# A bilinear interaction kernel: x in a ring loaded two blocks at a time, products in place, engine orders as written

One core of one Trainium2 chip. The metric is the device time of one execution in microseconds, smaller is better. Times are medians of several executions, all with nothing else on the core.

## The reference

Every row of the batch has 32 vectors of 64 numbers. For each of the 496 pairs i < j, vector i is multiplied by the pair's own 64 x 64 matrix and the result, number by number, by vector j.

```python
# inputs: r_inputs (4096, 32, 64) f32, L0_rec_W (496, 64, 64) f32
idx_i, idx_j = np.triu_indices(32, k=1)
vi = inputs[:, idx_i, :]
vj = inputs[:, idx_j, :]
vidots = jnp.einsum('bpd,pde->bpe', vi, W)
return vidots * vj          # (4096, 496, 64) f32: 520 MB
```

## The kernel before

128 rows form a row tile, two row tiles (k = 0, 1) a block, 16 blocks the batch. A row tile's 496 pairs are cut into five groups; a group is computed into one of three output buffers (`ot`) and stored with one DMA of 2.9 to 3.4 MB. x comes in blocks, W is transposed once at the start ("order" rearranges a chunk, "turn" transposes it on TensorE). Seven of the 46 product steps of a row tile go "aside": ScalarE (ACT) copies the matmul result out of PSUM, GpSimd (POOL) multiplies. The others are multiplied by VectorE (DVE) straight from PSUM.

```python
xpool = ctx.enter_context(tc.tile_pool(name="xpool", bufs=2))
xtpool = ctx.enter_context(tc.tile_pool(name="xtpool", bufs=4))
tpool = ctx.enter_context(tc.tile_pool(name="tpool", bufs=4))
opool = ctx.enter_context(tc.tile_pool(name="opool", bufs=3))
psum = ctx.enter_context(tc.tile_pool(name="psum", bufs=4, space=bass.MemoryType.PSUM))
# ... (cut)
def order_w(c: int, k: int, copy):
    r = wrows[c][1] - wrows[c][0]
    rp = tpool.tile([P, EU, 2, D], F32, tag="tmp", name=f"rp_{c}_{k}")
    src = raw[c][:r, :].rearrange("p (d h e) -> p e h d", h=2, d=D)
    copy(rp[:r], src[:, k * EU : (k + 1) * EU])
    return rp
# ... (cut: turn_w, turn_x)
LEAD = 3    # the first three row tiles go group by group, the others one after the other
sched = [(t, s) for g in range(len(groups)) for t in range(LEAD) for s in range(NS) if steps[s][0] == g]
sched += [(t, s) for t in range(LEAD, NT) for s in range(NS)]
# ... (cut)
for c, orders, turns in (                     # at which step a quarter of a W chunk is
    (1, (2, 4, 8, 10), (4, 7, 12, 15)),       # ordered and turned
    (2, (17, 22, 27, 32), (19, 24, 29, 34)),  # chunk 2 is ordered on POOL
    (3, (54, 54, 55, 55), (57, 60, 63, 66)),
):
    ...
no_aside = range(52, 67)
# ... (cut: the loop over sched; per step the matmuls into ps, then)
if i in aside and c0 == 0 and s not in no_aside:
    tmp = tpool.tile([P, CH, 2, E2], F32, tag="tmp", name=f"tmp_{s}")
    nc.scalar.copy(tmp, src)
    nc.gpsimd.tensor_mul(dst, tmp, xj)
else:
    nc.vector.tensor_mul(dst, src, xj)
# after a group's last step: nc.sync.dma_start(out rows <- ot)
```

## Time and profile before

| | before |
|---|---|
| time | 1354.68 us (1354.08 to 1354.79) |
| span of the profiled execution | 1353.3 us |
| DMA | 562.9 MB, 416 GB/s over the span |
| PE, DVE, POOL, ACT busy | 87, 71, 39, 28% |
| stores | 161 on one queue, 520 MB |

The share of DMA engines busy is in tenths over 40 slices of the span, and it is 9 in all but the last; no compute engine comes near that. The lines themselves stand in the prediction. The trace also has a record of every DMA packet (queue, size, start, length, but no engine number); where this text says "packet records", its numbers were worked out from those.

### The profile page before, as it was taken

What the parts mean: (1) busy time and instruction counts of PE and PEld (TensorE: products, weight loads), DVE (VectorE), ACT (ScalarE), POOL (GpSimd) and SP (SyncE); (2) the same over time, 40 slices, a digit from 0 to 9 for tenths busy, and PEclk for the clock granted to TensorE, in tenths of its full rate; (3) what the DMA queues carried; (4) which work ended last, traced back from release to release, by engine and by line L of the source; (5) the groups of instructions that cost most, each with busy time, mean ns of one, the idle gap of its engine ahead of it and who ended that gap; (6) DMA issues with size and microseconds to landing.
All of it is one profiled execution on the core that took longest, in us unless ns stands there. A gap on an engine that the chain in (4) does not pass through costs nothing.

```text
span 1353.3 us, 17856 instructions
## 1 busy us (share of the span) xinstructions
PE 1180.3 (87%) x7424; PEld 690.9 (51%) x7424; DVE 956.9 (71%) x1262; ACT 374.1 (28%) x367; POOL 530.2 (39%) x246
## 2 busy tenths in 40 slices
PE   6989889889799897988879989888987989988994
PEld 4556545545455454555445545454554545545552
DVE  5778768767677676776757777676775767767774
ACT  3432222222232232222222222222222222223221
POOL 1813424444243443433444334433434434344431
PEclk9989999989999898999989999899998999989997
DMA  9999999999999999999999999999999999999997
GB/s 386 370 426 408 424 427 431 428 432 431 418 414 419 433 412 418 422 413 426 428 407 422 417 425 410 423 421 407 425 410 426 419 422 427 401 432 428 415 417 319
DMA packets 26273, 562.92 MB, mean 416 GB/s; under 512 B 2912, under 2 KB 2912, under 8 KB 3040
## 3 DMA queue, kind: packets, MB, share of 16 engines
q1 hardware_dynamic: 24048, 530.59, 92.4%
q10 hardware_dynamic: 2144, 31.20, 5.5%
q8 instruction: 58, 0.95, 0.3%
q14 instruction: 23, 0.19, 0.0%
HBM read 41.68 MB, written 520.09 MB: 415 GB/s over the span
## 4 chain that ended last, share of the span: by engine, by line
DMA 50%; PE 25%; DVE 17%; POOL 3%; issue 2%; ACT 0%; DVEq 0%; SPq 0%; POOLq 0%; ACTq 0%
DMA out_dram<-ot 50%; PE ps L211 20%; DVE ot L228 17%; PE ptx L114 4%; POOL ot L226 3%; PE ptw L104 1%; DMA raw<-in_L_rec_W_dram 1%; ACT tmp L225 0%; DVE rp L95 0%; POOL rp L95 0%; DVEq L228 0%; ACT wT L107 0%; SPq L76 0%; POOLq L226 0%; SPq L233 0%
## 5 line engine op out<-in xcount | busy, mean ns | idle before, releaser
L228 DVE TENSOR_TENSOR ot<-ps,xs 128x1024 f32<-128x1024 f32 (+15 forms) x1252 | 945.6, 808 | 364.7 <-DMA out_dram<-ot 185.9
L211 PE MATMUL ps<-wT,xT 64*128 64x512 f32 (+13 forms) x6272 | 1034.9, 473 | 132.8 <-DVE ot L228 121.3
L211 PEld LDWEIGHTS ps<-wT,xT 64*128 64x128 f32 x6272 | 563.7, 197 | 569.9 <-DVE ot L228 306.8
L226 POOL TENSOR_TENSOR ot<-tmp,xs 128x1024 f32<-128x1024 f32 x220 | 519.6, 2362 | 647.4 <-ACT tmp L225 457.1
L225 ACT COPY tmp<-ps 128x1024 f32<-128x1024 f32 x220 | 222.7, 1012 | 500.1 <-PE ps L211 459.6
L118 ACT COPY xT<-ptx 128x1024 f32<-128x1024 f32 x128 | 129.6, 1012 | 428.2 <-PE ptx L114 428.2
L114 PE MATMUL ptx<-ident,xs 128*128 128x128 f32 x1024 | 141.2, 281 | 18.5 <-DVE ot L228 9.9
L114 PEld LDWEIGHTS ptx<-ident,xs 128*128 128x128 f32 x1024 | 111.0, 142 | 64.3 <-issue 44.1
L72 POOL MEMSET xs<- 128x64 f32 x16 | 2.4, 152 | 148.6 <-DVE ot L228 148.6
L104 PE MATMUL ptw<-ident,rp 128*128 128x128 f32 (+1 forms) x128 | 19.2, 305 | 3.9 <-DVE rp L95 3.9
L104 PEld LDWEIGHTS ptw<-ident,rp 128*128 128x128 f32 (+1 forms) x128 | 16.2, 160 | 10.3 <-DVE rp L95 5.0
L107 ACT COPY wT<-ptw 128x1024 f32<-128x1024 f32 (+1 forms) x15 | 14.8, 984 | 21.4 <-PE ptw L104 21.4
L95 DVE COPY rp<-raw 128x1024 f32<-128x1024 f32 (+1 forms) x9 | 10.7, 1219 | 11.1 <-DMA raw<-in_L_rec_W_dram 11.1
L95 POOL COPY rp<-raw 128x1024 f32<-128x1024 f32 x4 | 8.0, 1994 | 0.1
L95 ACT COPY rp<-raw 112x1024 f32<-112x1024 f32 (+1 forms) x3 | 5.9, 1959 | 5.1 <-POOL ot L226 3.3
L107 DVE COPY wT<-ptw 128x1024 f32<-128x1024 f32 x1 | 1.2, 1224 | 3.3 <-PE ptw L104 3.3
L118 ACT ACT_TABLE_LOAD x1 | 1.3, 1283 | 0.7 <-PEq L251 0.7
masks.py:197 POOL MEMSET ident<- 128x128 f32 x1 | 0.2, 206 | 0.3 <-POOLq L251 0.3
masks.py:199 POOL TENSOR_SCALAR_AFFINE_SELECT ident<-ident 128x128 f32<-128x128 f32 x1 | 0.3, 295 | 0.0
L251 POOL MEMSET const-float32-0.0<- 128x1 f32 x1 | 0.1, 99 | 0.2 <-issue 0.2
L251 POOL MEMSET const-bfloat16-1.0<- 128x1 bf16 x1 | 0.1, 102 | 0.0
L251 POOL MEMSET const-uint8-127<- 128x1 uint8 x1 | 0.1, 102 | 0.0
(1 smaller groups left out, 0.1 us busy)
## 6 DMA issues: line engine op xcount, KB each, us to landing
out_dram<-ot SPq DMA_DIRECT2D x64, 3360.0 KB, 16.2
out_dram<-ot SPq DMA_DIRECT2D x32, 3168.0 KB, 15.4
out_dram<-ot SPq DMA_DIRECT2D x32, 3104.0 KB, 17.0
out_dram<-ot SPq DMA_DIRECT2D x31, 2880.0 KB, 16.4
xs<-in_r_inputs_dram ACTq DMA_DIRECT2D x14, 2048.0 KB, 16.6
raw<-in_L_rec_W_dram SPq DMA_DIRECT2D x3, 2048.0 KB, 14.3
xs<-in_r_inputs_dram SPq DMA_DIRECT2D x2, 1024.0 KB, 10.9
xs<-in_r_inputs_dram SPq DMA_DIRECT2D x1, 2048.0 KB, 24.6
```

What stands on the lines that cost most here:

```text
L72: nc.gpsimd.memset(xs[blk][:, 0, :], 0.0)
L95: copy(rp[:r], src[:, k * EU : (k + 1) * EU])
L104: nc.tensor.transpose(pt[:, n, :r], rp[:r, n].rearrange("p h d -> p (h d)"), ident[:r, :r])
L107: copy(wT[c][:, :, k * EU : (k + 1) * EU], pt[:, :, :r].rearrange("p e r -> p r e"))
L114: nc.tensor.transpose(pt[:, n, :], xs[blk][:, s : s + 2, :].rearrange("p f d -> p (f d)"), ident)
L118: copy(xT, pt)
L211: nc.tensor.matmul(ps[:, h, lo - pa : hi - pa, :], xT[blk, kt, n // RUN][h * D : (h + 1) * D, n % RUN, :], wT[c][h * D : (h + 1) * D, lo - ...
L225: nc.scalar.copy(tmp, src)
L226: nc.gpsimd.tensor_mul(dst, tmp, xj)
L228: nc.vector.tensor_mul(dst, src, xj)
L251: nc = _bacc.Bacc("TRN2", target_bir_lowering=False, num_devices=1)
```

## The change

x sits in one ring of three blocks, and two neighbouring blocks come by one load of 4 MB; where the ring puts the pair in swapped places, rows of the two blocks swap roles. The place of the ring that the first two blocks leave free (the middle one) holds the rearranged W at the start, so no temporary tiles are left. The last chunk of W is now loaded at step 36; before, its load stood behind the last copy of chunk 2, at step 32. An aside product is copied into the output buffer and multiplied there. No step is exempt from going aside. The instructions of each engine run in the order of the source, where before a scheduler ordered them.

```diff
-    xpool = ctx.enter_context(tc.tile_pool(name="xpool", bufs=2))
-    tpool = ctx.enter_context(tc.tile_pool(name="tpool", bufs=4))
+    NX = 3
+    xs = const.tile([P, 1 + NX * NB * F, D], F32, tag="xs", name="xs")
+    def slot(blk: int, k: int, i: int = 0) -> int:
+        c, n = divmod(blk, 2)
+        b = 1 - n if c % 2 else 2 * n if c == 0 else 1 + n
+        return 1 + (b * NB + k) * F + i
+    def load_two(blk: int, eng):
+        ...                                   # cut: one DMA for blocks blk, blk + 1
+        eng.dma_start(out=dst[:, b : b + 2, :], in_=src)
@@ order_w
-        rp = tpool.tile([P, EU, 2, D], F32, tag="tmp", name=f"rp_{c}_{k}")
+        rp = xs[:, 1 + NB * F : 1 + 2 * NB * F, :].rearrange("p (n e h) d -> p n e h d", e=EU, h=2)[:, k]
@@ steps of ordering, loads
-        (1, (2, 4, 8, 10), (4, 7, 12, 15)),
+        (1, (0, 0, 2, 6), (4, 7, 12, 15)),
-    no_aside = range(52, 67)
+    LAST_W = 36                               # the last chunk of W is loaded at this step
-    loads = {place[blk * NB, LATE]: blk + 1 for blk in range(2, NBLK - 1)}
-    loads[place[LEAD, LATE]] = 2
+    loads = {place[LEAD, LATE]: 2}
+    for blk in range(3, NBLK - 1, 2):
+        loads[place[blk * NB, LATE]] = blk + 1
+    ctx.enter_context(tc.manual_schedule())
@@ the product
-        if i in aside and c0 == 0 and s not in no_aside:
-            tmp = tpool.tile([P, CH, 2, E2], F32, tag="tmp", name=f"tmp_{s}")
-            nc.scalar.copy(tmp, src)
-            nc.gpsimd.tensor_mul(dst, tmp, xj)
+        if i in aside and c0 == 0:
+            nc.scalar.copy(dst, src)
+            nc.gpsimd.tensor_mul(dst, dst, xj)
```

More of the change, by code (lines that the diff above doesn't have):

```diff
@@ L62, with rows_in @@
     make_identity(nc, ident)
-    xs = {}
+    NX = 3
+    xs = const.tile([P, 1 + NX * NB * F, D], F32, tag="xs", name="xs")
+    nc.gpsimd.memset(xs[:, 0, :], 0.0)
     def rows_of(dram: bass.AP, blk: int) -> bass.AP:
         return dram[blk * NB * P : (blk + 1) * NB * P]
-    def new_x(blk: int):
-        xs[blk] = xpool.tile([P, 1 + NB * F, D], F32, tag="xs", name=f"xs_{blk}")
-        nc.gpsimd.memset(xs[blk][:, 0, :], 0.0)
-    def load_x(blk: int, eng, k0: int = 0, k1: int = NB):
-        src = rows_of(x, blk).rearrange("(p k) f d -> p (k f) d", k=NB)
-        eng.dma_start(out=xs[blk][:, 1 + k0 * F : 1 + k1 * F, :], in_=src[:, k0 * F : k1 * F, :])
+    def slot(blk: int, k: int, i: int = 0) -> int:
+        c, n = divmod(blk, 2)
+        b = 1 - n if c % 2 else 2 * n if c == 0 else 1 + n
+        return 1 + (b * NB + k) * F + i
+    def rows_in(dram: bass.AP, blk: int) -> bass.AP:
+        return rows_of(dram, blk ^ (blk // 2 % 2))
+    def load_x(blk: int, eng, k0: int = 0, k1: int = NB):
+        src = rows_in(x, blk).rearrange("(p k) f d -> p (k f) d", k=NB)
+        eng.dma_start(
+            out=xs[:, slot(blk, k0) : slot(blk, k1 - 1) + F, :], in_=src[:, k0 * F : k1 * F, :]
+        )
+    def load_two(blk: int, eng):
+        n = NB * F
+        dst = xs[:, 1:, :].rearrange("p (b n) d -> p b (n d)", n=n)
+        b = min(slot(blk, 0), slot(blk + 1, 0)) // n
+        src = x[blk * NB * P : (blk + 2) * NB * P].rearrange("(b p k) f d -> p b (k f d)", b=2, k=NB)
+        eng.dma_start(out=dst[:, b : b + 2, :], in_=src)
     wflat = w.rearrange("p d e -> p (d e)")
@@ L112, in turn_x @@
         for n in range(RUN):
-            s = k * F + q * RUN + n
+            s = slot(blk, k, q * RUN + n) - 1
             nc.tensor.transpose(
-                pt[:, n, :], xs[blk][:, s : s + 2, :].rearrange("p f d -> p (f d)"), ident
+                pt[:, n, :], xs[:, s : s + 2, :].rearrange("p f d -> p (f d)"), ident
             )
@@ L158 @@
             due.setdefault(turns[k], []).append(("turn", c, k))
-    no_aside = range(52, 67)
+    LAST_W = 36
     LATE = 6
-    loads = {place[blk * NB, LATE]: blk + 1 for blk in range(2, NBLK - 1)}
-    loads[place[LEAD, LATE]] = 2
-    new_x(0)
+    loads = {place[LEAD, LATE]: 2}
+    for blk in range(3, NBLK - 1, 2):
+        loads[place[blk * NB, LATE]] = blk + 1
     load_x(0, nc.sync, 0, 1)
@@ L169 @@
     load_w(2)
-    new_x(1)
     load_x(1, nc.sync)
+    ctx.enter_context(tc.manual_schedule())
     v, p, a = nc.vector.tensor_copy, nc.gpsimd.tensor_copy, nc.scalar.copy
@@ L185 @@
         g, i, c0, m = steps[st]
+        if s == LAST_W:
+            load_w(3, nc.scalar)
         if s in loads:
-            new_x(loads[s])
-            load_x(loads[s], nc.scalar)
+            load_two(loads[s], nc.scalar)
         for what, *args in due.get(s, ()):
@@ L196 @@
                 rps[c, k] = order_w(c, k, (v, v, p, v)[c] if k % 2 == 0 else (v, v, p, a)[c])
-                if (c, k) == (2, NU - 1):
-                    load_w(3, nc.scalar)
         base, end = groups[g]
@@ L218 @@
         o = pa - base
-        j = 1 + kt * F + i + 1 + c0
+        j = slot(blk, kt, i + 1 + c0)
         dst = ot[:, o : o + m, :].rearrange("p m (h e) -> p m h e", h=2)
         src = ps[:, :, :m, :].rearrange("p h m e -> p m h e")
-        xj = xs[blk][:, j : j + m, :].rearrange("p m (h e) -> p m h e", h=2)
-        if i in aside and c0 == 0 and s not in no_aside:
-            tmp = tpool.tile([P, CH, 2, E2], F32, tag="tmp", name=f"tmp_{s}")
-            nc.scalar.copy(tmp, src)
-            nc.gpsimd.tensor_mul(dst, tmp, xj)
+        xj = xs[:, j : j + m, :].rearrange("p m (h e) -> p m h e", h=2)
+        if i in aside and c0 == 0:
+            nc.scalar.copy(dst, src)
+            nc.gpsimd.tensor_mul(dst, dst, xj)
         else:
@@ L233 @@
             nc.sync.dma_start(
-                out=rows_of(out, blk).rearrange("(p k) n d -> p k n d", k=NB)[:, kt, n0 : pa + m, :],
+                out=rows_in(out, blk).rearrange("(p k) n d -> p k n d", k=NB)[:, kt, n0 : pa + m, :],
                 in_=ot[:, n0 - base : pa + m - base, :],
```

## The prediction

> **What bounds the kernel now.** I read the page's header, busy shares and DMA rows first, then the stretches, then the waits, and last the start of the chain that ended last. The page:
>
> ```profile
> span 1353.3 us, 17856 instructions
> PE 1180.3 (87%) x7424; PEld 690.9 (51%) x7424; DVE 956.9 (71%) x1262; ACT 374.1 (28%) x367; POOL 530.2 (39%) x246
> DMA  9999999999999999999999999999999999999997
> DMA packets 26273, 562.92 MB, mean 416 GB/s; under 512 B 2912, under 2 KB 2912, under 8 KB 3040
> q1 hardware_dynamic: 24048, 530.59, 92.4%
> q10 hardware_dynamic: 2144, 31.20, 5.5%
> ```
>
> No engine is full, and the 16 DMA engines are: q1 (stores, W and the first x) and q10 (x loads issued by ACT, and the last part of W) together take 97.9% of 16 engines' span. The bytes are the output's, so they can't shrink. In the trace's packet records the commonest store packet, 26880 bytes, takes 996 ns, 27.0 bytes/ns. An engine's share is 562.92/16 = 35.18 MB, 1303 us at that rate. So some 50 us of the span are not plain transfer. The stretches say where some lie (us from the start; the last columns are granted clock, DMA share, GB/s):
>
> ```profile
> 0.00:27.00 27.00, 15.66 (x82) 11.51 (x84) 11.16 (x11) 10.35 (x9) 3.28 (x9) 1.00 0.94 388
> 27.00:60.00 33.00, 33.00 (x199) 18.74 (x196) 24.78 (x25) 15.19 (x15) 23.38 (x11) 1.00 0.92 378
> 60.00:104.00 44.00, 40.22 (x255) 25.55 (x253) 32.93 (x41) 17.55 (x16) 12.76 (x7) 0.88 0.97 399
> 104.00:140.00 36.00, 35.51 (x250) 21.52 (x248) 30.50 (x48) 8.10 (x8) 9.53 (x5) 1.00 1.00 418
> 340.00:1340.00 1000.00, 880.09 (x5526) 510.80 (x5524) 714.17 (x950) 268.28 (x265) 398.31 (x179) 0.95 0.99 419
> 1345.00:1351.00 6.00, 0.00 (x0) 0.00 (x0) 0.00 (x0) 0.00 (x0) 0.00 (x0) 0.50 0.07 31
> ```
>
> The start, to about 104 us, is short of stores and PE is full in it (20.00 of 20 us, 33.00 of 33). The last row is the surprise: for 6 us the DMA share is 0.07, about one engine in sixteen (0.0625). The packet records agree: at the end most engines are done near 1344.3 us, one goes on to 1350.4. Following that one back: around 500 us it moves 23040 bytes in 860 to 898 ns where the others take 855, and 24832 in 935 to 982 where they take 921, with no gap between packets. **One DMA engine is 3 to 4% slower per packet.** Its distance behind the others grows from 1 us at 160 us to about 6 us at 330 us, and then stays there: an output buffer is free only when the slowest sixteenth of its store is done, so the other fifteen wait for it. The chain's starts of the matching stores confirm the pace: 431.27 and 514.33, 83.1 us for two row tiles of five stores each. At 27 bytes/ns the two tiles' 34.6 MB would be 80.1 us. So from about 104 us on the end is set by that engine's own work, whatever the compute engines do, as long as it never runs dry. That compute is ahead of it:
>
> ```profile
> DVE ot L228 <- DMA out_dram<-ot: 185.9, 84, 5.8
> POOL ot L226 <- DMA out_dram<-ot: 153.1, 59, 5.5
> ACT tmp L225 <- POOL ot L226: 36.1, 9, 5.0
> ```
>
> DVE waits 84 times for an output buffer, 186 us over 32 row tiles, 5.8 us a tile.
>
> **What the Trainium skill says.** (1) "DMA: Bandwidth & Descriptors", section "Latency and other measured facts": engines 7 and 15 are usually slower in traces, with a guessed cause tied to software descriptor rings. This trace has one slow engine; its records carry no engine number, and all queues that matter here are hardware ones, so the guessed cause does not fit. (2) Same page, "Measured": 425 GB/s for a 16 MB load on a lone core; the trace has 430 between 140 and 340 us. There is no rate left for larger loads to win. (3) Same page, "Issuing engines are not separate DMA queues": loads from ACT and stores from SP share the 16 engines and interleave. The trace agrees: while a load runs, packets of 16384 bytes (611 ns) and of 26880 alternate on the slow engine. So two blocks in one load move the same packets over the same engines.
>
> **The change, part by part.**
>
> *Loads.* 14 loads of 2 MB become 7 of 4 MB; packets stay 16 KB, 128 per block. Each issue costs ACT about 0.4 us, beside the path. I looked for a cost at each start of a load: stores' packets are late by 0.3 to 0.8 us there, but on the fast engines, which had just been idle (they have run out of stores); on the slow engine packets are only 50 to 70 ns late. Saving: 0 to 1 us. A pair arrives two tiles (about 83 us) less some steps before its first use, as before, and the order of instructions shows no new wait for a load. Expected cost 0. The 14 further memsets (0.15 us each) also go, off the path.
>
> *Aside products.* 220 become 224: ACT copy 1.01 us, POOL product 2.36 us. Four DVE products of 1.22 us move away, all in steps 52 to 66, where PE is the limit: about 0. The copies now go to the output buffer, so ACT itself waits for a store, in order, and transposed x behind it waits too. PE gets one or two PSUM steps less far ahead at the start of a group; I estimate 1 us a group, 4 us a tile, against DVE's 5.8 us of waiting. The slow engine has a queued store of some 8 us when a buffer comes free. So 0 in the end.
>
> *Orders.* PE's order is the same line for line, and DVE's differs in a handful of rows of the start. On POOL each of the four W reorderings for rows 256 to 383 moves behind one more product. The chain there was:
>
> ```profile
> 43.40 2.37 POOL ot L226
> 45.76 1.84 issue
> 47.64 2.35 POOL ot L226
> 49.99 1.94 POOL rp L95
> 51.92 2.33 POOL ot L226
> 56.12 2.42 POOL ot L226
> 58.55 16.29 DMA out_dram<-ot
> ```
>
> I redo it with the new order, ACT copy 1.01 us after the product, POOL 2.36, reordering 1.97. First reordering: POOL is free at 41.4, done 43.3; PE came for it at 42.3: PE 1.0 us late. Second: done 47.8, PE there at 48.0: nothing. Third: its product waits for a copy until 52.0 and ends at 54.4, reordering done 56.4, PE there at 53.0: 3.4 late, 4.5 in all. Fourth: product 59.8 to 62.2, reordering to 64.2, PE there at 61.5: about 7 us in all. The store issued at 58.55 then comes near 62.2, and DMA is empty some 3 us before it; the last load of W goes at about 66 in place of 56, which mends part of that. Of PE's 7 us, 4.8 are taken from waits it had anyway between 72 and 81 us (44.00 - 40.22 = 3.8 idle in its stretch, and about 1 hidden in matmuls that waited), where all engines waited for a store that I expect at the same time as before, near 75 us. **Left: about 2.5 us.** PE is full from 81 to 135 us and the store at 103.6 found DMA just empty, so this goes to the end one for one.
>
> Sum: 0 to -1 from loads, 0 from aside products, +2.5 from orders: 1354.7 + 2.5 = about 1357 us.
>
> **Rivals.** (a) *Fewer turns between reads and writes make DMA faster.* For it: packets are late near starts of loads, and the share of 0.99 hides small gaps. Against it: the lateness is not on the slow engine. If it were real, 7 starts at 0.5 us: -3.5 us, so 1351. (b) *ACT in order becomes a wait.* For it: ACT now stands at a group's start where DVE stood, with copies of transposed x behind it; slack was 5.8 us a tile. If it costs more than that by 1.5 us a tile over 29 tiles, +44 us: 1399. Against it: PE needs only 1180.3/32 = 36.9 us a tile of the slow engine's 41.5, and the wait stops as soon as compute falls behind. (c) *A pair of loads holds up stores.* It puts 16 load packets on each engine (256 over 16), which alternate with store packets: some 16 x (0.62 + 1.03) = 26 us in which stores run at 62% of their rate and buffers come free later, in place of two times 13 us. Against it: the engine is never empty meanwhile, and afterwards all three buffers stand full: 0. (d) *The slow engine is slow because of where a buffer lies or which engine reads it.* Nothing shows it; if moving buffers cured it, 41 us less: about 1315.
>
> **Range and chances.** The orders' term is +2.5 with 4 us of doubt either way (my redoing of the start), loads -3.5 to 0, ACT's waits 0 to +5: 1349 to 1365. Faster by over 2% needs under 1327.6, which only (d) gives: 0.02. Slower by over 2% needs over 1381.8, by (b): 0.04. Within 2%: 0.94.
>
> **What would show it.** Right: DMA share 1.00 or 0.99 from 104 us on, again a single engine working for about 6 us at the end, about 83 us for two tiles; stores of the second group some 1, 4 and 7 us later; PE waiting for POOL's reordering near 53 and 62 us; ACT now listed as waiting for stores, at no cost. Wrong: a pace other than 83 us for two tiles. Shorter says that reads and writes mattered or that the slow engine changed; longer, with idle on that engine, that ACT's order has taken the bound.

## The result, and the profile after

The changed kernel takes **1360.0 us** (1359.7 to 1361.88, 4 runs) beside 1354.46 us for the kernel before in the same rounds. The ratio is 1.0044, with a 95% interval of 1.0027 to 1.0061. (Ratios here are the mean time of one kernel's fast runs over that of the other's fast runs of the same rounds, so not quite the ratio of the medians.) By the 2% measure it is the same; clear of noise it is 5.5 us slower. The spans of the two profiled executions differ by 4.6 us.

The page of the changed kernel: header, DMA, then groups of instructions (busy time, mean ns of one; idle time before them and what ended most of it).

```profile
span 1357.9 us, 17899 instructions
PE 1147.9 (85%) x7424; PEld 673.1 (50%) x7424; DVE 950.6 (70%) x1258; ACT 378.1 (28%) x371; POOL 537.6 (40%) x235
DMA packets 26162, 562.93 MB, mean 415 GB/s; under 512 B 2800, under 2 KB 2800, under 8 KB 2928
L242 POOL TENSOR_TENSOR ot<-ot,xs 128x1024 f32<-128x1024 f32 x224 | 529.4, 2363 | 793.3 <-ACT ot L241 789.6
L241 ACT COPY ot<-ps 128x1024 f32<-128x1024 f32 x224 | 226.8, 1013 | 554.1 <-DMA out_dram<-ot 348.3
xs<-in_r_inputs_dram ACTq DMA_DIRECT2D x7, 4096.0 KB, 29.6
```

Bytes and the lengths of single instructions are as before: POOL's product in place 2363 ns (2362 before), the copy 1013 ns (1012). ACT now waits for output buffers, 348.3 us in all, which it did not do before. That is a large new wait, and the question is whether it costs anything. Here are three stretches of the changed kernel, to be compared with those that the prediction shows (last columns: clock, DMA share, GB/s):

```profile
104.00:140.00 36.00, 35.51 (x256) 21.72 (x252) 31.00 (x50) 8.10 (x8) 10.64 (x5) 1.00 1.00 428
340.00:1340.00 1000.00, 859.41 (x5578) 500.97 (x5576) 717.27 (x957) 271.34 (x268) 402.14 (x171) 0.97 0.99 419
1350.00:1356.00 6.00, 0.00 (x0) 0.00 (x0) 0.00 (x0) 0.00 (x0) 0.00 (x0) 0.50 0.06 27
```

From 340 to 1340 us both move 419 GB/s at a share of 0.99, and at the end a single engine again works alone for 6 us (0.06). The times at which stores are issued confirm it: between stores 59 and 139 (counted from 0), eight pairs of row tiles, the kernel before takes 662.06 us and the changed one 661.99 us, 82.75 us a pair in both. ACT's 348 us of waiting cost nothing.

So the difference lies before. DMA in the start, the kernel before first:

```profile
27.00:50.00 23.00, 23.00 (x134) 12.70 (x132) 17.72 (x18) 10.16 (x11) 13.38 (x7) 1.00 0.89 377
50.00:60.00 10.00, 10.00 (x67) 6.03 (x64) 7.06 (x8) 5.03 (x5) 10.00 (x5) 1.00 0.98 381
60.00:76.00 16.00, 12.64 (x85) 7.71 (x85) 9.47 (x13) 7.90 (x7) 8.95 (x5) 0.97 0.99 385
```

and the changed kernel:

```profile
27.00:50.00 23.00, 21.95 (x128) 12.30 (x129) 16.48 (x17) 10.13 (x10) 13.03 (x6) 1.00 0.90 379
50.00:60.00 10.00, 6.69 (x36) 3.96 (x34) 3.56 (x5) 3.04 (x3) 4.43 (x4) 0.83 0.75 320
60.00:76.00 16.00, 14.00 (x92) 8.37 (x90) 10.14 (x11) 6.30 (x7) 11.37 (x6) 1.00 0.83 293
```

PE (first busy column) was full from 50 to 60 us, and is idle for 3.3 of the 10 now; DMA falls from 381 to 320 and from 385 to 293 GB/s. In the packet records DMA runs dry twice: from about 50.1 to 51.5 us most or all of the engines stand empty, and from 59.1 to 63.2 us nearly all or all of them do. Together this is worth 5.7 us of all 16 engines, where before the one gap there was worth 0.4. What PE waited for in the changed kernel (waits of 36 to 106 us: total, times, longest):

```profile
PEld ptw L121 <- POOL xs L112: 8.7, 4, 3.9
PE ptw L121 <- POOL xs L112: 6.3, 3, 3.3
```

in the kernel before, over the whole execution:

```profile
PEld ptw L104 <- POOL rp L95: 0.5, 1, 0.5
```

and, again in the changed kernel, POOL's own row of work (start, length, what; in brackets idle before):

```profile
47.87 2.36 POOL L242 TENSOR_TENSOR ot<-ot,xs 128x1024 f32<-128x1024 f32 x1 [0.97 <-ACT ot L241]
51.39 2.35 POOL L242 TENSOR_TENSOR ot<-ot,xs 128x1024 f32<-128x1024 f32 x1 [1.16 <-ACT ot L241]
53.69 1.89 POOL L112 COPY xs<-raw 128x1024 f32<-128x1024 f32 x1
59.98 2.35 POOL L242 TENSOR_TENSOR ot<-ot,xs 128x1024 f32<-128x1024 f32 x1 [4.41 <-ACT ot L241]
62.28 1.92 POOL L112 COPY xs<-raw 128x1024 f32<-128x1024 f32 x1
64.15 2.36 POOL L242 TENSOR_TENSOR ot<-ot,xs 128x1024 f32<-128x1024 f32 x1
```

Compare with the chain that the prediction shows: there the copies (reorderings of W) of 49.9 and 54.2 us were done about when PE came for them (it waited for 0.5 us). Now each stands behind one more product, which waits for ACT, which waits for PE, which waits for the copy before: a circle of engines that the kernel before did not have. The issues of stores 4, 5 and 6 (the second group of the three first row tiles) move from 50.40, 58.55 and 65.32 us to 50.69, 62.36 and 72.60 us.

### The profile page after: what moved, and what is told of

It reads as the page before. It is cut to its first block, busy times and chain, and to the rows that moved or that the text cites. A ratio compares the mean times of both kernels' runs of the same rounds, so it can differ in the third digit from the quotient of the medians.

```text
span 1357.9 us, 17899 instructions
## 1 busy us (share of the span) xinstructions
PE 1147.9 (85%) x7424; PEld 673.1 (50%) x7424; DVE 950.6 (70%) x1258; ACT 378.1 (28%) x371; POOL 537.6 (40%) x235
## 4 chain that ended last, share of the span: by engine, by line
DMA 54%; PE 19%; DVE 16%; issue 4%; POOL 3%; ACT 3%; DVEq 0%; ACTq 0%; SPq 0%; POOLq 0%
DMA out_dram<-ot 53%; DVE ot L244 16%; PE ps L228 14%; PE ptx L131 4%; POOL ot L242 3%; ACT ot L241 2%; ACT xT L135 1%; PE ptw L121 0%; POOL xs L112 0%; DMA xs<-in_r_inputs_dram 0%; DVE xs L112 0%; DVEq L244 0%; SPq L249 0%; ACTq L135 0%; ACTq L241 0%
## 5 line engine op out<-in xcount | busy, mean ns | idle before, releaser
L228 PE MATMUL ps<-wT,xT 64*128 64x512 f32 (+13 forms) x6272 | 1000.1, 461 | 94.9 <-DVE ot L244 82.3
L242 POOL TENSOR_TENSOR ot<-ot,xs 128x1024 f32<-128x1024 f32 x224 | 529.4, 2363 | 793.3 <-ACT ot L241 789.6
L228 PEld LDWEIGHTS ps<-wT,xT 64*128 64x128 f32 x6272 | 546.4, 191 | 513.7 <-DVE ot L244 241.4
L241 ACT COPY ot<-ps 128x1024 f32<-128x1024 f32 x224 | 226.8, 1013 | 554.1 <-DMA out_dram<-ot 348.3
L135 ACT COPY xT<-ptx 128x1024 f32<-128x1024 f32 x128 | 129.6, 1012 | 379.4 <-PE ptx L131 379.3
L121 PE MATMUL ptw<-ident,xs 128*128 128x128 f32 (+1 forms) x128 | 18.3, 295 | 10.2 <-POOL xs L112 6.3
L121 PEld LDWEIGHTS ptw<-ident,xs 128*128 128x128 f32 (+1 forms) x128 | 15.2, 153 | 16.9 <-POOL xs L112 8.7
L112 DVE COPY xs<-raw 128x1024 f32<-128x1024 f32 (+1 forms) x9 | 11.2, 1274 | 10.8 <-DMA raw<-in_L_rec_W_dram 10.8
L112 POOL COPY xs<-raw 128x1024 f32<-128x1024 f32 x4 | 7.7, 1934 | 0.0
L112 ACT COPY xs<-raw 112x1024 f32<-112x1024 f32 (+1 forms) x3 | 5.8, 1984 | 1.8 <-DMA raw<-in_L_rec_W_dram 1.8
```

What stands on the lines that cost most here:

```text
L121: nc.tensor.transpose(pt[:, n, :r], rp[:r, n].rearrange("p h d -> p (h d)"), ident[:r, :r])
L135: copy(xT, pt)
L228: nc.tensor.matmul(ps[:, h, lo - pa : hi - pa, :], xT[blk, kt, n // RUN][h * D : (h + 1) * D, n % RUN, :], wT[c][h * D : (h + 1) * D, lo - ...
L241: nc.scalar.copy(dst, src)
L242: nc.gpsimd.tensor_mul(dst, dst, xj)
```

## The experiments

Theory: the order of four copies on POOL starves DMA in the start, and everything else of the change is neutral, because one slow DMA engine sets the pace. Rivals: the products in place (ACT's waits), the pairs of loads, the lateness of the first load of x, or a bound that DMA shares with compute. Each run is timed in five rounds beside the kernel before (medians 1354.3 to 1354.6 us). Two tables of results come first, the edits and expectations after.

| run | base | time us | ratio to before, 95% |
|---|---|---|---|
| e1_scheduler | changed, scheduler on | 1362.94 | 1.0064 (1.0051 to 1.0077) |
| e2_pool_order | changed, POOL's order mended | 1354.83 | 1.0001 (0.9989 to 1.0014) |
| e3_all_early | e2, and W's last chunk and first pair early | 1354.89 | 1.0006 (0.9994 to 1.0018) |
| e4_before_source_order | before, orders as written | 1363.41 | 1.0064 (1.0052 to 1.0077) |
| e5_bf16 | changed, bf16 matmuls | 1348.89 | 0.9963 (0.9951 to 0.9975) |
| e6_fifteen | changed, a fifth of the stores cut 120 + 8 | 1733.24 | none, see there |
| e7_single_loads | changed, 14 single loads | 1360.67 | 1.0046 (1.0032 to 1.0059) |
| e8_first_pair_early | changed, first pair early | 1360.33 | 1.0044 (1.0031 to 1.0056) |
| e9_eight_rows | e5, extra loads to 8 partitions | 1366.20 | 1.0089 (1.0075 to 1.0103) |
| e10_sixteen_rows | e5, extra loads to 16 partitions | 1367.21 | 1.0098 (1.0082 to 1.0113) |

When the last engine is done with a store, from the packet records, in us. Store 7 is the first of the third group; "difference" is against the kernel before.

| | store 7 | difference | last store (160) | difference |
|---|---|---|---|---|
| before | 89.2 | | 1351.2 | |
| changed | 94.3 | +5.1 | 1356.1 | +4.9 |
| e2_pool_order | 89.5 | +0.3 | 1351.2 | 0.0 |
| e3_all_early | 88.9 | -0.3 | 1350.7 | -0.5 |
| e4_before_source_order | 97.0 | +7.8 | 1358.9 | +7.7 |
| e7_single_loads | 95.0 | +5.8 | 1356.9 | +5.7 |
| e8_first_pair_early | 94.8 | +5.6 | 1356.4 | +5.2 |
| e1_scheduler | 94.0 | +4.8 | 1359.4 | +8.2 |

**e1_scheduler.** The scheduler is switched back on.

```diff
-    ctx.enter_context(tc.manual_schedule())
```

> The changed kernel with the scheduler switched back on; ring, paired loads and products in place stay. On POOL the W reorderings then stand ahead of the products again, one place earlier even than in the kernel before, and the last load of W goes out earlier on ACT. My theory (the order of the start on POOL and the late DMAs cost 4.6 us of the span, the rest of the change nothing): between 1353 and 1356 us. Rival (products in place, with ACT waiting for stores in order, cost it): stays at 1360. Rival (paired loads cost it): stays at 1360.

Measured 1362.94 us: slower still. This was a miss. The scheduler of this version does not restore the old order. It moves two copies of W and the last load of W too far forward, and DVE's copy of that chunk to a place where it waits for the landing (waits of 30 to 80 us):

```profile
POOL ot L241 <- issue: 12.5, 1, 12.5
PE ptw L121 <- DVE ot L243: 9.0, 1, 9.0
DVE xs L112 <- DMA raw<-in_L_rec_W_dram: 8.5, 1, 8.5
```

So "scheduler on" is not "order of before", and this run cannot tell the parts of the change apart; e2 and e4 do. It also lost 3.4 us after store 7, the only run of that table that did so: from store 59 to 139 it takes 664.81 us, 83.1 us for two row tiles in place of 82.75. Why, stays open.

**e2_pool_order.** Four numbers are edited, which puts each of POOL's copies before the product that it had fallen behind.

```diff
-        (2, (17, 22, 27, 32), (19, 24, 29, 34)),
+        (2, (14, 18, 25, 29), (19, 24, 29, 34)),
```

> The changed kernel with only the four reorderings of W rows 256 to 383 written earlier, at steps 14, 18, 25, 29 in place of 17, 22, 27, 32, which gives POOL the order of the kernel before. My theory: the DMA gaps before the second and third store of the second group (1.4 and 4.2 us of all 16 engines) close, but the last load of W and the first load of x stay late: 1356 to 1358 us. If the order on POOL has no part in it: 1360.

Measured 1354.83 us, ratio 1.0001: the whole loss is gone, more than expected (1356 to 1358). (The gaps named there precede the first and second store of the second group, not the second and third; I had misread their place.) The ring, the pairs, the products in place and ACT's waits for stores (347.4 us) are all still there, and the first load of x is still late (146.5 us; 135.3 before, 150.1 in the changed kernel). The last load of W is not: it goes out at 58.2 us (56.2 before, 65.4 in the changed kernel), though its step was not edited. Most of its lateness was thus itself an effect of POOL's order, and this run mends both. The stretches of this run:

```profile
50.00:60.00 10.00, 10.00 (x67) 6.01 (x66) 7.09 (x8) 5.06 (x5) 10.00 (x6) 1.00 0.98 378
60.00:76.00 16.00, 12.72 (x84) 7.42 (x81) 9.29 (x13) 5.81 (x6) 7.89 (x4) 0.97 0.97 386
```

PE is full again from 50 to 60 us and DMA is back at 378 and 386 GB/s, as in the kernel before.

**e4_before_source_order.** The kernel before with source order and nothing else.

```diff
+    ctx.enter_context(tc.manual_schedule())
     v, p, a = nc.vector.tensor_copy, nc.gpsimd.tensor_copy, nc.scalar.copy
```

> The kernel before with engine orders as in its source and nothing else of the change. POOL then has the changed kernel's order of reorderings and products. My theory: slower than before by nearly the whole loss, 1357 to 1360 us. If the ring, the pairs or the products in place carry the loss: 1354 to 1355.

Measured 1363.41 us, 8.8 us slower, beyond what was expected. POOL's copies and products stand in the changed kernel's order, so source order brings a loss without any other part of the change. (It puts all engines in source order; that POOL's is the one that counts is shown by e2.) It costs more here: four temporary tiles serve both the copies of W and the aside products, and ACT's copies wait for them (7.0 us for POOL's rearranged W between 36 and 106 us; the changed kernel has no such wait). That the ring as a place for W saves this difference fits, but was not tried alone.

**e7_single_loads.** Loads of one block into the same ring.

```diff
-    for blk in range(3, NBLK - 1, 2):
+    for blk in range(2, NBLK - 1):
         loads[place[blk * NB, LATE]] = blk + 1
-            load_two(loads[s], nc.scalar)
+            load_x(loads[s], nc.scalar)
```

> The changed kernel with 14 loads of one block into the same ring in place of 7 of two. My theory: the same packets on the same engines, so 1359 to 1361 us, equal to the changed kernel within 1 us. Rival (each start of a load costs DMA some 0.5 us): 3 to 4 us slower, 1363 to 1364. Rival (a pair holds stores up): faster than the changed kernel by 1 us or more.

Measured 1360.67 us against 1360.0 us for pairs: seven more loads cost no more than 0.7 us together, and the rival of 0.5 us at each start falls. The second table even has all of the 0.7 us at store 7, long before the first of these loads (149 us); from there to the end this run loses nothing more than the changed kernel.

**e3_all_early.** e2, and the last chunk of W and the first pair of x earlier.

```diff
-        (2, (17, 22, 27, 32), (19, 24, 29, 34)),
+        (2, (14, 18, 25, 29), (19, 24, 29, 34)),
-    LAST_W = 36
+    LAST_W = 30
-    loads = {place[LEAD, LATE]: 2}
+    loads = {place[LEAD - 1, NS - 14 + LATE]: 2}
```

> As the run with POOL's order mended, and the last load of W at step 30 in place of 36, and the first pair of x two row tiles' groups earlier (in the third tile's last group, where the scheduler of the kernel before had put its first load). My theory: all of the loss is in these three places, so 1353 to 1355.5 us, equal to before. If ACT's waits for stores or the pairs cost something of their own: 1357 or more.

Measured 1354.89 us: equal to e2 and to before. It is within what was expected, but the two added edits gain nothing that can be told from noise. With POOL's order mended the load of W had only 2 us left to gain (56.2 us for 58.2); on the changed kernel as it stands an earlier load of W was not tried.

**e8_first_pair_early.** Only the last of these edits, on the changed kernel.

> The changed kernel with nothing moved but the first pair of x, issued in the third row tile's last group. The changed kernel lost 2.8 us against before until store 10 (POOL's order) and 2.1 us more between stores 16 and 25. My theory: those 2.1 us are DMA that ran empty near 148 us because the first load of x came 15 us later; filled early, they come back: 1357.5 to 1359 us. If they have another cause (the pair itself, ACT's waits): 1360.

Measured 1360.33 us: no gain, and my explanation of "2.1 us between stores 16 and 25" falls. I had followed the times at which stores are issued, which say when compute is done. The second table follows the slowest DMA engine, and there the changed kernel is 5.1 us late at store 7 and 4.9 us late at the end: nothing is lost between, and there is nothing for an earlier load to give back.

**e5_bf16.** PE's work is cut down by keeping both operands of the product matmuls in bf16 (less exact on purpose).

```diff
-        xT = xtpool.tile([P, RUN, P], F32, tag="xT", name=f"xT_{blk}_{k}_{q}")
+        xT = xtpool.tile([P, RUN, P], mybir.dt.bfloat16, tag="xT", name=f"xT_{blk}_{k}_{q}")
-            wT[c] = const.tile([P, r, E2], F32, tag=f"w{c}", name=f"wT_{c}")
+            wT[c] = const.tile([P, r, E2], mybir.dt.bfloat16, tag=f"w{c}", name=f"wT_{c}")
```

> The changed kernel with transposed x and W kept in bf16 (less exact on purpose): the matmuls of the products take far less of PE. My theory: from 104 us on one slow DMA engine sets the time, so the pace stays at 82.7 us for two row tiles and only the start gains, where PE was full: 1340 to 1352 us. Rival (PE and compute share the bound in the steady part): the pace falls to the 80.1 us of plain transfer, some 40 us less: 1310 to 1325.

Measured 1348.89 us. Its page and its steady stretch:

```profile
PE 785.5 (58%) x4288; PEld 395.8 (29%) x4288; DVE 937.7 (70%) x1258; ACT 371.5 (28%) x371; POOL 535.3 (40%) x235
340.00:1330.00 990.00, 583.62 (x3164) 287.20 (x3163) 705.69 (x953) 264.32 (x266) 396.80 (x169) 0.57 0.99 421
```

PE loses 362 us of busy time (1147.9 to 785.5) and the kernel 11 us. The steady rate goes from 419 to 421 GB/s. Compute is not the bound there. But "only the start gains" was wrong: at store 7 this run is 4.0 us ahead of the changed kernel (90.3 us for 94.3), at the last store 10.8 us (1345.3 for 1356.1), so more than half of the gain comes later. In the steady part it is some 0.3 us of each pair of row tiles (82.46 for 82.75). Some 42% of PE's instructions are gone and with them 25 of 58 fetches of instructions by DMA, but whether that is the cause was not tried.

**e9_eight_rows and e10_sixteen_rows.** On e5's base, one useless load per row tile from the fourth on.

```diff
+        if st == 3 and t >= LEAD:
+            nc.scalar.dma_start(
+                out=extra[:8, :], in_=x[:16].rearrange("(p k) f d -> p (k f d)", k=2)
+            )                    # e10: extra[:16], x[:32]
```

> The bf16 version (1348.9 us) with one more load per row tile from the fourth on (29 in all), 16 KB to each of partitions 0 to 7, never read. By the Trainium skill (DMA: Bandwidth & Descriptors, why a DMA increments its semaphore by 16) such a load runs on 8 engines, the lowest-numbered. A packet of 16 KB takes 611 ns: 17.7 us more on those 8 engines, none on the others. If one slow engine among the upper 8 sets the time: 1348 to 1351 us. If the slow one is among the lower 8: 1364 to 1370. If the 16 engines' summed rate sets it: 29 x 131 KB at 432 GB/s, 8.8 us: 1356 to 1360.

> The same with 16 rows, so on all 16 engines. Any theory in which DMA sets the time: 17.7 us more, 1364 to 1370 us. If DMA had slack: 1349 to 1355.

Measured 1366.2 and 1367.21 us, 17.3 and 18.3 us above e5. (e5 ran in other rounds; the kernel before took 1354.33 us there and 1354.45 here.) Eight rows cost about as much as sixteen, though they are half the bytes. If the 16 engines' common rate were the bound, eight rows would have cost half. So it is the busiest engine that counts, and by the rule that the Trainium skill states for the number of engines ("DMA: Bandwidth & Descriptors", "Why a DMA increments its semaphore by 16 and not by 1": a load to 8 partitions runs on the eight lowest-numbered) it is one of the lower eight. The trace agrees on the number, with eight packets of 16 KB for each such load; which engines they are it does not say. One reservation: the extra packets of e9 took some 814 ns rather than 611, so some 23.6 us on each of the eight. Had the slow engine been in the upper half, the loaded eight would first have had to make up what it has more to do than they, and only the rest of the 23.6 us would have cost time. The packet records speak against this. In e5 an engine stands empty for 13.9 us on average between 104 and 1335 us. If the slow one never does, it has some 15 us more to do than the others, and the cost would have been some 9 us (an estimate from these numbers), not 17.3. And at store 100 of e9 eight engines are done within 0.1 us of each other, seven more from 1.4 us later on, and the slow one 6.7 us later: with those seven it makes up the loaded eight. (At some other stores the first group has seven.) e10 by itself does not show a slow engine: between 104 and 1352 us its engines stand empty for only 0.5 us on average, and its extra packets took 905 ns.

**e6_fifteen.** Every fifth store is cut in two.

```diff
-            nc.sync.dma_start(
-                out=rows_in(out, blk).rearrange("(p k) n d -> p k n d", k=NB)[:, kt, n0 : pa + m, :],
-                in_=ot[:, n0 - base : pa + m - base, :],
-            )
+            for q0, q1 in ((0, 120), (120, P)) if g == len(groups) - 1 else ((0, P),):
+                nc.sync.dma_start(... [q0:q1, kt, n0 : pa + m, :], in_=ot[q0:q1, n0 - base : pa + m - base, :])
```

> The changed kernel with the last store of each row tile (32 of 161) cut in two, partitions 0 to 119 and 120 to 127. By the Trainium skill (DMA: Bandwidth & Descriptors, how many engines) the first then runs on 15 engines and the second on 8, both counted from the lowest, so the 16th engine has no part in a fifth of the stores. Theory that the slow engine is the 16th and bounds the time: its work falls by some 20%, the others' rises by 1 to 3%, and the time falls by 15 to 30 us, to 1330 to 1345, with nothing left over at the end by a single engine. If the slow engine is another one: it gets 1.3% or more on top: 1375 to 1395 us. If no single engine is the bound: 1360 to 1375.

Measured 1733 us (1645 to 1754): no theory had this, and the run is inconclusive for its question. Packets of 26880 bytes, the size of the cut stores and of those before them, took 1411 ns on average in place of 1017 in the changed kernel; between 340 and 1300 us a third of them took 2170 ns on average and the others 1032. The profile was marked slow by the spread of its runs, so only the order of magnitude is used. The trace has 15 and 8 semaphore writes for the two parts of a cut store, as the rule has it. A store cut in 120 and 8 partitions is far slower than a whole one here; why, and which part does it, was not tried. e9 later put the slow engine among the lower eight, which this cut would not have relieved anyway.

## Why the prediction was right

The time, 1360.0 us, lies in the range of 1349 to 1365; the centre, 1357, is 3.0 us low.

- **Bound: one slow DMA engine from about 104 us on.** Right. The pace of 82.75 us for two row tiles is the same before and after, the lone engine at the end is there in both, taking 362 us off PE changed it by 0.3%, and e9 and e10 show that the busiest engine counts and not the sum. It even holds from earlier than 104 us: delays at store 7 (89 us) reach the end to within 0.4 us in every run but e1, e6 and those with bf16.
- **The size of that engine's lag: 3 to 4%, and 41 us in rival (d).** Too large. It was measured against the commonest packet, and the packets of all engines are longer than that on average (26880 bytes: 1020 ns for 996 in the kernel before). By the packet records an engine stands empty for 20.8 us on average between 104 us and the end of the last store. If the slow one never does, that is 22 us for each of the other 15: so much more work it has than they, 1.8%, and so much a cure could give at most if nothing else changed (an estimate). Nor is it always slow. Once compute has ended (1336.0 us before, 1341.0 us after), its packets of 26880 bytes take 996 to 1001 ns, like the commonest, after one of 1020 ns in the changed kernel, while the other engines still work. Just before, its packets of 25344 bytes took 954 to 1001 ns, where the commonest is 940. What slows it beside compute was not tried.
- **Loads in pairs: 0 to -1 us.** Right: 0.7 us between e7 and the changed kernel, and none of it after store 7.
- **Aside products in place: 0.** Right: e2 keeps them and takes 1354.83 us. ACT does wait, for 348.3 us, about 10.9 us a row tile, and at no cost. My estimate of 4 us a tile was of lost lead and not of this wait; no run measured it by itself.
- **Orders: PE late by 1.0, 0, 3.4, and 7 us in all.** Right in kind and nearly in size. PE's waits for the copies add up to 6.3 us. The store predicted near 62.2 us came at 62.36, the last load of W predicted at 66 us went out at 65.4.
- **What is left of it: +2.5 us.** This term was too small: it came to 4.9 us, as the second table shows. The step that failed is "PE is full from 81 to 135 us and the store at 103.6 found DMA just empty, so this goes to the end one for one". That followed PE's delay, which did come out at 2.8 us in the store at 103.6 (106.44 after). But the slow engine, which I had named as the bound, loses when DMA is empty, and it lost its time at 50 to 52 and 59 to 63 us, whatever compute caught up later. I had seen "DMA is empty some 3 us before it", and let the late load of W mend it; measured, the two gaps are 5.7 us for 0.4 before, and the load went out at 65.4 us, after the second gap, and so could fill none of it. That the sum still fell into the range is owed to the 4 us of doubt that this term was given.
- **Rivals.** (a) faster by fewer turns between reads and writes: refuted by e7. (b) ACT in order as a bound: refuted by e2. (c) pairs holding up stores: no sign of it, the pace is the same. (d) a cure of the slow engine by moving buffers: did not happen, the lone engine remains, and a cure could have given some 22 us at most, not 41.
- **Small slips that change nothing.** Most engines are done near 1345.0 us and the last at 1351.2 us, not 1344.3 and 1350.4; 7 less 4.8 us leaves 2.2, not 2.5; 15 memsets go, not 14.

No version beat the kernel before within float32: e2 and e3 equal it (1354.83 and 1354.89 us). What the change lacked was four step numbers.

## What to carry to other kernels

When DMA sets the time, follow the slowest engine's work from start to end: here time that it stood empty at the start (5.1 us at store 7, 4.9 us at the end) was lost for good, while waits of compute that a full queue covered (348 us on ACT) cost nothing. When orders are taken over by hand from a scheduler, compare each engine's order with the scheduler's around every instruction that another engine will wait for. A changed kernel with its scheduler back on is not a control, since the scheduler answers to the other edits as well; edit the one order in question.

## What the Trainium skill lacked or had wrong

- "DMA: Bandwidth & Descriptors", "Latency and other measured facts": engines 7 and 15 are said to be usually slower, with a guess at software descriptor rings. Here all queues that matter are hardware ones, and one engine is slow all the same (around 500 us packets of 860 to 898 ns for 855). e9 and e10 speak for one of the lower eight (17.3 us for 8 rows, 18.3 us for 16). The page gives no size: here it runs 6 us behind most others, has some 22 us more work than they in 1247, and is not slow once compute has ended.
- Same page, "Why a DMA increments its semaphore by 16 and not by 1": the rule for the number of engines fits the numbers of packets and semaphore writes in e9 and e6. The skill advises 128 partitions for a DMA, but no page gives a figure from which the cost of e6 would follow: cutting a fifth of the stores into 120 and 8 partitions took the time from 1360 to 1733 us, and packets of 26880 bytes from 1017 to 1411 ns on average.
